# Sums taken up at the head of each four slots in a gather-and-sum loop

## The chip, the cores and the metric

The kernel runs on one core of a Trainium2 chip, in one launch. The metric is the time of one execution in microseconds. The kernel before was run three times: 5961.7, 5947.33 and 5960.33, with a median of 5960.33. The profile shows one more execution of it.

In the profile the engines are called PE (TensorE: matrix products), PEld (the load of the stationary operand, which overlaps PE), DVE (VectorE), ACT (ScalarE), POOL (GpSimd) and SP (the engine that starts most plain transfers). Each works through its own queue, and they wait for each other by semaphores.

## What is computed

A graph has 12,500 nodes with 256 features and 200,000 edges, and the edges come sorted by target. Three layers of mean aggregation run over it; a linear attention and a mixture of eight experts follow, and the kernel computes these too. The part around the change is this:

```python
def _sage_conv(x, src, dst, Wl, bl, Wr, num_nodes):
    msg = x[src]
    s = jax.ops.segment_sum(msg, dst, num_segments=num_nodes)
    cnt = jax.ops.segment_sum(jnp.ones((msg.shape[0],), x.dtype), dst, num_segments=num_nodes)
    agg = s / jnp.maximum(cnt, 1.0)[:, None]
    return agg @ Wl.T + bl + x @ Wr.T
...
h = _sage_conv(x, src, dst, Wl0, bl0, Wr0, n)
h = jax.nn.leaky_relu(h, LEAKY_SLOPE)
h = _sage_conv(h, src, dst, Wl1, bl1, Wr1, n)
h = jax.nn.leaky_relu(h, LEAKY_SLOPE)
h = _sage_conv(h, src, dst, Wl2, bl2, Wr2, n)
```

## The kernel before: slots, take-ups and what is woven between them

**Slots.** The sorted edges are cut into slots of at most 128 edges that all point into one block of 128 target nodes. There are 98 blocks, walked from the last to the first, so that the ones with few edges come first. For a slot, `gather` lets POOL start an indirect DMA that brings the 128 source rows into a message tile (`msgs`, a ring of `MSGS` = 32 tiles in the first two layers). `make_hots` lets DVE compare target numbers with a row of column numbers, for four slots at a time (`FEW` = 4); the result, `hots`, is a matrix of zeros and ones per slot. `product` multiplies the two on PE and adds the result to the sums of the slot's block. The sums (`acc`) lie in PSUM, in a ring of 4 blocks in the first layer (`layer` 0) and of 6 in the second. In the first layer the message tile has one column more, filled with ones, so that the last column of the sums is the count of edges. The first two layers take 1240 slots each in this way; the six densest blocks are summed by another way, from matrices of counts that DVE and PE build during the first layer (class `Counts`, lines 1115 to 1260: sorting by `MAX8` and `MATCH_REPLACE8`, then comparisons into `src_hot` and `dst_hot`, then products `p_n`). `MSGS` appears in the waiting steps of that counting too (`all_sorted`), beside its use as the ring's size.

**The loop of the first two layers** (after the return of the `if e` branch in `on_the_way_of`) does four slots per iteration. In the program's order an iteration at slot `s` is:

1. the four gathers (POOL);
2. the product of slot `s + 3` (PE), which waits for the youngest of the four messages;
3. `stage(0)`, one step of the work that follows finished sums (`products`: transposes, the two linear maps, their evictions by ACT and DVE), then `stage(1)`, one step of independent work (`first_products` in the first layer, `attended` in the second);
4. `make_hots` for slot `s + 12` (DVE, line 1374);
5. `take_up` of every block whose due slot is `s` (DVE, lines 1428 to 1438);
6. the loads of `h` that are due (`ask`);
7. the products of slots `s`, `s + 1`, `s + 2` (PE, line 1402), and after each of them one or two steps of the counting (DVE, PE and POOL) or, later, of the dense sums.

**take_up** reads a finished sum out of PSUM and clears it. In the first layer it has four instructions on DVE: the maximum of the count and 1 (line 1428), the reciprocal (1429), the scaling into the tile `mean` (1430) and the clearing of the sum (1438). Lines 1430 and 1438 are put into a group, `evicts`, on which products are told not to wait; line 1428, which also reads the sums, isn't put into it. The clearing is waited for by the first product of the next iteration (`cleared`, with `BACK` = 4). In the second layer a take-up is lines 1434 and 1438 alone, both in the group, and blocks are taken up in pairs. When the last block of a group is taken up, its `products` are appended to the queue `soon`, from which `stage(0)` draws.

**Reuse of tiles.** `hots` has `HOTS + 1` = 4 buffers of four slots in the pool `work`; the one for slot `s + 12` was last read by the products of the iteration before. `mean` has two buffers in the same pool. The gather of slot `s` (a multiple of 4) waits for the last product that reads the tile of slot `s - 32`. The third layer (`e` is set) has a loop of its own.

Of the kernel before, what the change touches and what calls it, by code (L numbers as in the profile page):

```python
# [41 lines left out]
F32 = mybir.dt.float32  # L42
BF = mybir.dt.bfloat16
# [12 lines left out]
P = 128  # L56
D = 256
# [5 lines left out]
G = 4  # L63
# [3 lines left out]
W = D + 1  # L67
AHEAD = 8
EARLY = 16
MSGS, PARTED = 32, 24  # L70
FEW = 4
HOTS = 3
BACK = 4
# [13 lines left out]
def gps_kernel(ctx: ExitStack, tc: tile.TileContext, x, src, dst, wlr, bl, wq, wk, wv,  # L87
# [15 lines left out]
    for r0, r1, most in ((0, SMALL, G), (SMALL, NB, 2)):  # L103
        for r in range(r0, r1, most):
            n = min(most, r1 - r)
# [169 lines left out]
    with ExitStack() as first:  # L275
        sort = first.enter_context(tc.tile_pool(name="sort", bufs=1))
        work = first.enter_context(tc.tile_pool(name="work", bufs=2))
        psum = first.enter_context(tc.tile_pool(name="psum1", bufs=1, space=PSUM))
# [27 lines left out]
        for c in range(NCH):  # L306
            s = slice(c * CW, (c + 1) * CW)
# [118 lines left out]
        for c in range(KC):  # L426
            n = min(P, NK - c * P)
# [591 lines left out]
    def open_pool(stack, name, **kw):  # L1019
        return stack.enter_context(tc.tile_pool(name=name, **{"bufs": 1, **kw}))  # L1020

    def take_messages(lists, n):

        msgs = [lists.tile([P, W], F32, name=f"msg{i}") for i in range(n)]
        for msg in msgs:
            nc.vector.memset(msg[:, D:], 1.0)
        return msgs
# [45 lines left out]
    def on_the_way():  # L1073


        with ExitStack() as stack:
            lists = open_pool(stack, "lists_w")
            work = open_pool(stack, "work_w", bufs=2)
            inv = lists.tile([P, NB], F32, name="inv_w")

            tables = [where, lists.tile([1, NS], I32, name="where1")]
            nc.vector.tensor_scalar(tables[1], where, 43.0, None, op0=OP.mult)
            nc.vector.tensor_scalar(tables[1], tables[1], 8, None, op0=OP.logical_shift_right)
            nc.vector.scalar_tensor_tensor(tables[1], tables[1], -float(RING[1]), where,
                                           op0=OP.mult, op1=OP.add)
            nc.vector.tensor_scalar(tables[1], tables[1], float(D), None, op0=OP.mult)
            nc.vector.tensor_scalar(where, where, RING[0] - 1, None, op0=OP.bitwise_and)
            nc.vector.tensor_scalar(where, where, 2.0 * D, None, op0=OP.mult)
            a = Attention(lists)
            stack.enter_context(tc.manual_schedule())  # L1090
            with ExitStack() as two:
                msgs = take_messages(open_pool(two, "messages"), MSGS)
                for layer in range(2):
                    with ExitStack() as own:
                        psum = open_pool(own, f"psum_w{layer}", space=PSUM)
                        on_the_way_of(layer, tables[layer], due[FEWER - 1], work, psum, inv, msgs,
                                      a, Counts(own), None)
            parted = open_pool(stack, "parted")
            msgs = [parted.tile([P, 3 * D], BF, name=f"msg_parts{i}") for i in range(PARTED)]
            psum = open_pool(stack, "psum_w2", space=PSUM)  # L1100
            e = Experts(open_pool(stack, "big"), work, psum)
            e.parted = parted
            nc.vector.tensor_scalar(where, where, 0.5, None, op0=OP.mult)
            c = Counts(stack)
            c.work = open_pool(stack, "sums2")
            on_the_way_of(2, where, due[MORE - 1], work, psum, inv, msgs, a, c, e)

    class Counts:
# [240 lines left out]
        def tile(self, shape, dtype, name, tag=None, bufs=None):  # L1349
            return self.pool.tile(shape, dtype, name=name, tag="any", bufs=self.bufs)  # L1350

    def on_the_way_of(layer, table, last, work, psum, inv, msgs, a, c, e):


        blocks = MORE if e else FEWER
# [4 lines left out]
        hots, made_of, cleared, taken, zs, at, at_of = {}, {}, {}, {}, {}, (), -1  # L1360
        rows_of = {}
        now, soon, later, made, left = [None, None], deque(), deque(), set(), {}
        whole = psum.tile([P, 2 * D], F32, name="whole", tag="whole")
        if layer == 0:
            psum = OneTag(psum, 3)
# [3 lines left out]

        def make_hots(s):  # L1370
            n = min(FEW, last - s)
            hot = (e.parted if e else work).tile([P, FEW, P], BF if e else F32, name="hots",
                                                 bufs=HOTS + 1)
            nc.vector.tensor_tensor(  # L1374
                hot[:, :n, :], cols.rearrange("p (o c) -> p o c", o=1).to_broadcast([P, n, P]),
                dst_of[:, s:s + n].rearrange("p (n o) -> p n o", o=1).to_broadcast([P, n, P]),
                OP.is_equal)
            for i in range(n):
                hots[s + i] = hot[:, i, :]
# [35 lines left out]
        def take_up(r, sums=None):  # L1415

            g = group_of[r]
            b, n = falling[g]
            j = NB - 1 - r - b
            by_slots = sums is None  # L1420
            if by_slots:
                sums = sums_of(r)
            if layer == 0:
                if g not in taken:
                    taken[g] = (work.tile([P, G, D], F32, name="mean") if by_slots else
                                c.work.tile([P, G, D], F32, name="mean_c"))
                if by_slots:
                    nc.vector.tensor_scalar(inv[:, r:r + 1], sums[:, D:], 1.0, None, op0=OP.max)
                    nc.vector.reciprocal(inv[:, r:r + 1], inv[:, r:r + 1])
                got = nc.vector.tensor_scalar(taken[g][:, j, :], sums[:, :D],  # L1430
                                              inv[:, r:r + 1], None, op0=OP.mult)
            else:
                h = zs[g][:, j, :]
                got = nc.vector.scalar_tensor_tensor(h, sums, inv[:, r:r + 1], h,
                                                     op0=OP.mult, op1=OP.add)
            if by_slots:
                tc.add_to_no_dep_group(evicts, got.ins)
            got = nc.vector.memset(sums, 0.0)
            if by_slots:
                tc.add_to_no_dep_group(evicts, got.ins)  # L1440
                cleared.setdefault(when[r] + BACK, []).append(got.ins)
            left[g] = left.get(g, n) - 1
            if left[g]:
                return
            h = zs.pop(g)
            if layer == 1:
                nc.vector.scalar_tensor_tensor(h[:, :n, :], h[:, :n, :], SLOPE, h[:, :n, :],
                                               op0=OP.mult, op1=OP.max)
            if layer < 2:
                soon.append([-1, products(layer, b, n, taken.pop(g, h), h, work, psum,  # L1450
                                          parts=c.work if layer else None), True])
            else:
                nc.sync.dma_start(rows(z_tab[2], b, n), h[:, :n, :])
                e.ready.append((b, n))
# [108 lines left out]
        for s in range(0, last, FEW):  # L1563
            for i in range(FEW):
                gather(s + i)
            product(s + FEW - 1)
            stage(0)
            share = SHARE[layer] * (2 if counting and c.sorting else 1)
            credit = min(credit + share, 2 * share)
            if credit > 0:  # L1570
                credit -= stage(1) or 0.0
            if s + HOTS * FEW < last:
                make_hots(s + HOTS * FEW)
            while r < blocks and when[r] == s:
                take_up(r)
                r += 1
            while g < len(z_by) and z_by[g] <= s:
                ask(g)
                g += 1
            if counting is None and summing is None:  # L1580
                pace = n_steps / ((sums_to - s) / FEW * (FEW - 1))
                nc.vector.memset(whole, 0.0)
                c.work = open_pool(c.stack, f"sums{layer}")
                for k in range(len(z_by), NG):
                    ask(k)
                summing = c.sums(layer, whole, take_up)
            for i in range(FEW - 1):
                product(s + i)
                if counting:
                    for _ in range(2 if i == 0 else 1):  # L1590
                        if counting and next(counting, 0) == 0:
                            counting = None
                elif summing:
                    due_steps += pace
                    while done_steps < due_steps:
                        next(summing, None)
                        done_steps += 1
            made_of[s + FEW - 1] = made_of[s + FEW - 2]
# [2 lines left out]
            r += 1  # L1601
        for _ in summing:
            pass
        while stage(0) is not None or stage(1) is not None:
            pass

# [54 lines left out]
```

## Time and profile before

| | us |
|---|---|
| three runs, lowest / median / highest | 5947.33 / 5960.33 / 5961.7 |
| the profiled execution, its time | 5964.23 |
| the same, from the first to the last instruction (span) | 5961.5 |

The mean granted clock of PE over the span is 0.95. By the starts of line 1402 in the timeline the first layer's slots run from 193 to 2125 us, the second layer's from 2149 to 3757; the third layer and the experts take the rest. The page counts busy time by engine, then shows 40 slices of 149 us, the DMA queues, the chain that ended last, and the costliest groups of instructions: line, engine, operation, tile, count, then busy time and mean duration, then how long the engine sat idle just before and what ended most of that.

### The profile page before, as it was taken

The page shows a single profiled execution, that of the slowest core. Times are in us where ns is not written, and L with a number is a line of the kernel's source. Part 1 is how long each engine was busy: PE and PEld are TensorE (multiplying, and loading weights), DVE is VectorE, ACT ScalarE, POOL GpSimd, SP SyncE. Part 2 cuts the span into 40 slices and gives each one's busy share as a digit, 9 for nine tenths or more (in the row PEclk, how much of TensorE's full clock was granted, in tenths as well). Part 3 has the DMA queues.
Part 4 walks back from the last instruction along what each step waited for, and adds up shares of the span by engine and source line. Part 5 has one row for each costly group of instructions (what it writes and reads, how often), then busy time and mean ns, then how long its engine had stood idle before and what let it go on. Part 6 is the DMA issues. An engine that isn't in the chain of part 4 may idle for free. (4 is left out here: it accounts for less than half of the span.)

```text
span 5961.5 us, 75064 instructions
## 1 busy us (share of the span) xinstructions
PE 5080.2 (85%) x23992; PEld 3751.7 (63%) x23992; DVE 2605.2 (44%) x7130; ACT 1058.4 (18%) x1970; POOL 4084.3 (69%) x4146
## 2 busy tenths in 40 slices
PE   1677899989899978878777776599999999999999
PEld 0456666666787856656655555366666666666667
DVE  6637768676322233333332222244444444444433
ACT  3211111212000000000000000032233223322333
POOL 1677676777677767777777777666666666666661
PEclk9989999999999989999988888699999999999999
DMA  6545454456788867767765555556566656655551
GB/s 200 164 132 167 152 151 138 145 161 184 229 262 258 258 188 249 232 223 249 223 211 179 184 172 156 182 172 191 175 182 183 186 168 182 183 172 173 166 160 50
DMA packets 712593, 1101.62 MB, mean 185 GB/s; under 512 B 105872, under 2 KB 551334, under 8 KB 711964
## 3 DMA queue, kind: packets, MB, share of 16 engines
q0 software_dynamic: 213712, 604.20, 34.9%
q1 hardware_dynamic: 480927, 472.47, 24.4%
q10 hardware_dynamic: 17578, 20.04, 1.0%
q8 instruction: 223, 3.65, 0.3%
q14 instruction: 153, 1.25, 0.1%
HBM read 908.22 MB, written 188.11 MB: 184 GB/s over the span
## 5 line engine op out<-in xcount | busy, mean ns | idle before, releaser
L1382 POOL DMA_INDIRECT msg<-y,src_of x2480 | 2522.9, 1017 | 886.0 <-issue 660.0
L1402 PE MATMUL acc<-msg,hots 128*128 128x257 f32 (+1 forms) x4960 | 1413.1, 411 | 566.6 <-DMA msg<-y,src_of 379.2
L1382 POOL DMA_INDIRECT msg_parts<-y_parts,src_of x1404 | 1405.1, 1001 | 689.9 <-issue 347.6
L1402 PEld LDWEIGHTS acc<-msg,hots 128*128 128x128 f32 x4960 | 959.4, 203 | 842.9 <-issue 459.5
L1374 DVE TENSOR_TENSOR hots<-cols,dst_of 128x512 f32<-128x512 f32 (+1 forms) x971 | 663.7, 687 | 1242.1 <-PE acc L1402 1241.5
L976 PE MATMUL p_h<-turned,w_sb 128*128 128x512 f32 (+1 forms) x1728 | 754.7, 561 | 37.8 <-ACT hT L978 37.8
L1331 PE MATMUL whole<-y_c,count 128*128 128x256 f32 x2744 | 738.9, 394 | 16.4 <-DMA y_c<-y 8.6
L945 PE MATMUL p_y<-w_sb,hT 128*128 128x256 f32 x3136 | 748.0, 382 | 1.2 <-DVE x L932 1.1
L1402 PE MATMUL acc<-msg_parts,hots 128*128 128x256 bf16 x4212 | 631.7, 277 | 32.4 <-DMA msg_parts<-y_parts,src_of 18.7
L1402 PEld LDWEIGHTS <-hots 128*128 128x128 bf16 x4212 | 415.5, 100 | 360.7 <-issue 258.9
L945 PEld LDWEIGHTS p_y<-w_sb,hT 128*128 128x128 f32 x3136 | 571.4, 192 | 70.7 <-DVE x L932 1.6
L1331 PEld LDWEIGHTS whole<-y_c,count 128*128 128x128 f32 x2744 | 539.6, 200 | 95.8 <-issue 17.1
L932 DVE SCALAR_TENSOR_TENSOR x<-p_y,comb,x 128x256 f32<-128x256 f32 x784 | 340.5, 476 | 445.9 <-PE p_y L945 445.7
L664 ACT COPY turned<-p_tr 128x512 f32<-128x512 f32 (+1 forms) x270 | 137.7, 550 | 1953.8 <-PE p_tr L662 1853.1
L978 ACT ACTIVATE hT<-p_h,b_sb 128x512 f32<-128x512 f32 (+1 forms) x432 | 276.8, 647 | 1167.1 <-PE p_h L976 1162.2
L976 PEld LDWEIGHTS p_h<-turned,w_sb 128*128 128x128 f32 x1728 | 302.5, 193 | 227.1 <-issue 173.1
L248 PE MATMUL p_mm<-wlr_sb,turned 128*128 128x512 f32 x784 | 356.1, 597 | 0.5 <-ACT turned L664 0.5
L258 DVE TENSOR_TENSOR yz<-p_mm,bl_sb 128x256 f32<-128x256 f32 x196 | 80.7, 423 | 515.8 <-ACT y L257 257.0
L1212 DVE TENSOR_SCALAR src_hot<-nums,source_of 128x384 bf16<-128x384 uint16 x693 | 224.3, 324 | 123.8 <-PE p_n L1232 123.7
L1232 PE MATMUL p_n<-dst_hot,src_hot 128*128 128x256 bf16 x2058 | 266.8, 279 | 0.4 <-DVE dst_hot L1214 0.4
L248 PEld LDWEIGHTS p_mm<-wlr_sb,turned 128*128 128x128 f32 x784 | 150.4, 192 | 149.0 <-issue 130.1
L1232 PEld LDWEIGHTS <-src_hot 128*128 128x128 bf16 x2058 | 202.7, 100 | 57.0 <-issue 11.3
(301 smaller groups left out, 3840.4 us busy)
## 6 DMA issues: line engine op xcount, KB each, us to landing
count<-counts SPq DMA_DIRECT2D x294, 256.0 KB
y_c<-y SPq DMA_DIRECT2D x294, 256.0 KB
msg<-y,src_of POOLq DMA_INDIRECT x2480
counts<-counts_sb SPq DMA_DIRECT2D x96, 384.0 KB
h<-z SPq DMA_DIRECT2D x66, 512.0 KB
z<-yz SPq DMA_DIRECT2D x98, 256.0 KB
msg_parts<-y_parts,src_of POOLq DMA_INDIRECT x1404
y_parts<-y SPq DMA_DIRECT2D x49, 384.0 KB
```

The costliest lines, as they stand in the source:

```text
L248: nc.tensor.matmul(p, hT[:, k, j * P:(j + 1) * P], w[:, k, :], start=(k == 0), stop=(k == 1))
L664: nc.scalar.copy(tT[:, k, :n * P], p_tr[:, :n * P])
L932: nc.vector.scalar_tensor_tensor(xt[:, j, :], p[:, j - j0, :], comb[:, j, i:i + 1], xt[:, j, :], op0=OP.mult, op1=OP.add)
L945: nc.tensor.matmul(p[:, j - j0, :], hT[:, k, j * P:(j + 1) * P], e.w2[:, i, k, :], start=(k == 0), stop=(k == 1))
L976: nc.tensor.matmul(p_h[:, :n * P], e.w1[:, i, k, m * P:(m + 1) * P], tT[:, k, :n * P], start=(k == 0), stop=(k == 1))
L978: nc.scalar.activation(hT[:, m, :n * P], p_h[:, :n * P], AF.Gelu, bias=e.b1[:, i, m:m + 1])
L1212: nc.vector.tensor_scalar(src_hot[:, i, :], self.nums, source[:, c:c + 1], None, op0=OP.is_equal)
L1232: nc.tensor.matmul(p[:, t, :], s_hot[:, (t0 + t) * P:(t0 + t + 1) * P], d_hot, start=(i == 0), stop=(i == len(mine) - 1))
L1331: nc.tensor.matmul(acc[:, h * D:(h + 1) * D], c[:, j, h * P:(h + 1) * P], y[:, j, :], start=False, stop=True, skip_group_check=True)
L1374: nc.vector.tensor_tensor(hot[:, :n, :], cols.rearrange("p (o c) -> p o c", o=1).to_broadcast([P, n, P]), dst_of[:, s:s + n].rearrange("p ...
L1382: got = nc.gpsimd.indirect_dma_start(out=msgs[s % held] if e else msgs[s % held][:, :D], out_offset=None, in_=y_parts if e else y_tab[laye ...
L1402: got = nc.tensor.matmul(sums, hot, msgs[s % held][:, k * D:k * D + w], start=False, stop=True, skip_group_check=True)
```

## The change

Five edits, all for the first two layers:

- `take_up` of the blocks due at `s` moves from after `make_hots` to right after the four gathers, so ahead of the product of slot `s + 3`.
- A new queue `fresh` keeps the follow-up work of a take-up out of `soon` until after that iteration's `stage(0)`.
- `hots` has `HOTS + 2` = 5 buffers in place of 4.
- `hots` and `mean` of these layers move from the pool `work` to a new pool `early` with two buffers by default, which is closed with the messages.
- `MSGS` is 28 in place of 32.

```diff
-MSGS, PARTED = 32, 24
+MSGS, PARTED = 28, 24
...
                 msgs = take_messages(open_pool(two, "messages"), MSGS)
+                early = open_pool(two, "early", bufs=2)
...
+        fresh = []
...
-            hot = (e.parted if e else work).tile([P, FEW, P], BF if e else F32, name="hots",
-                                                 bufs=HOTS + 1)
+            hot = (e.parted if e else early).tile([P, FEW, P], BF if e else F32, name="hots",
+                                                  bufs=HOTS + (1 if e else 2))
...
-                    taken[g] = (work.tile([P, G, D], F32, name="mean") if by_slots else
+                    taken[g] = (early.tile([P, G, D], F32, name="mean") if by_slots else
...
-                soon.append([-1, products(layer, b, n, taken.pop(g, h), h, work, psum,
+                fresh.append([-1, products(layer, b, n, taken.pop(g, h), h, work, psum,
...
             for i in range(FEW):
                 gather(s + i)
+            while r < blocks and when[r] == s:
+                take_up(r)
+                r += 1
             product(s + FEW - 1)
             stage(0)
+            soon.extend(fresh)
+            fresh.clear()
...
                 make_hots(s + HOTS * FEW)
-            while r < blocks and when[r] == s:
-                take_up(r)
-                r += 1
...
         for _ in summing:
             pass
+        soon.extend(fresh)
         while stage(0) is not None or stage(1) is not None:
```

More of the change, by code (lines that the diff above doesn't have):

```diff
@@ L1096, in on_the_way @@
                         on_the_way_of(layer, tables[layer], due[FEWER - 1], work, psum, inv, msgs,
-                                      a, Counts(own), None)
+                                      a, Counts(own), None, early)
             parted = open_pool(stack, "parted")
@@ L1350, in tile, with on_the_way_of @@
             return self.pool.tile(shape, dtype, name=name, tag="any", bufs=self.bufs)
-    def on_the_way_of(layer, table, last, work, psum, inv, msgs, a, c, e):
+    def on_the_way_of(layer, table, last, work, psum, inv, msgs, a, c, e, early=None):
         blocks = MORE if e else FEWER
```

## The prediction

> **What bounds the kernel now.** I read the page first, then the table of windows over the stages, then the waits of POOL, PE and DVE window by window, and last the timeline around single take-ups.
>
> The page gives each engine's share, and the two halves of a slot:
>
> ```profile
> PE 5080.2 (85%) x23992; PEld 3751.7 (63%) x23992; DVE 2605.2 (44%) x7130; ACT 1058.4 (18%) x1970; POOL 4084.3 (69%) x4146
> ...
> L1382 POOL DMA_INDIRECT msg<-y,src_of x2480 | 2522.9, 1017 | 886.0 <-issue 660.0
> L1402 PE MATMUL acc<-msg,hots 128*128 128x257 f32 (+1 forms) x4960 | 1413.1, 411 | 566.6 <-DMA msg<-y,src_of 379.2
> ```
>
> A gather holds POOL for 0.95 us when undisturbed (0.95 in the timeline, 1.017 in the mean), and 0.30 us of issue follow: 1.25 us per slot is the fastest pace that the gathers allow. The windows part the stages (columns after the window: its length, then busy us and instructions of PE, PEld, DVE, ACT, POOL, then PE's clock, DMA share and GB/s):
>
> ```profile
> 450.00:745.00 295.00, 245.00 (x1160) 191.60 (x1161) 232.92 (x434) 47.50 (x102) 206.25 (x204) 0.93 0.52 159
> 745.00:1043.00 298.00, 272.50 (x1715) 205.60 (x1713) 223.30 (x738) 52.06 (x110) 207.49 (x180) 0.98 0.48 145
> ...
> 2130.00:3757.00 1627.00, 1236.41 (x4645) 933.75 (x4645) 500.09 (x910) 96.57 (x248) 1235.26 (x1240) 0.90 0.66 207
> ```
>
> **The second layer is paced by POOL.** Its 1240 gathers in 1627 us are 1.31 us each, near the 1.25 floor, and PE waits there for messages: the waits of PE from 2831 to 3428 are led by
>
> ```profile
> PE acc L1402 <- DMA msg<-y,src_of: 134.7, 56, 6.4
> ```
>
> **The first layer is paced by PE until about 1640 us.** From 450 to 1640 us POOL waits for the ring to come free, and from 450 to 1527 us PE waits for DVE's take-up (two answers: POOL's waits, then PE's):
>
> ```profile
> POOL msg L1382 <- PE acc L1402: 107.4, 44, 8.3
> ```
>
> ```profile
> PE acc L1402 <- DVE inv_w L1428: 101.1, 52, 5.4
> PE acc L1402 <- DMA msg<-y,src_of: 5.3, 2, 3.8
> ```
>
> Messages cost PE only 5.3 us in that stretch, and nothing from 550 to 1527, where the same view lists no wait for them. So PE's lost time passes on whole. From 1640 on POOL runs at its own pace (2.8 us of waits for PE from 1639 to 1937), and at 2095 to 2122 PE waits 1.4 to 3.7 us for messages in each iteration: the layer's end is POOL's. What reaches the end is when PE, about 1640 us, lets POOL go.
>
> **The wait that the change touches.** Line 1428 isn't in the group that products may ignore, so the next product in program order waits for it. Now that is the product of slot s; after the change it is that of slot s + 3, at the head. DVE works in order, so line 1428 comes when everything ahead of it on DVE is done. Now these are the evictions of both stages and `hots`; in the change, the counting steps of the iteration before. The timeline of one take-up (PE and DVE rows):
>
> ```profile
> 493.79 0.81 PE L1402 MATMUL acc<-msg,hots 128*128 128x257 f32 x3
> ...
> 494.44 1.89 PE L740 MATMUL p_z<-wlr_sb,turned 128*128 128x256 f32 x8
> ...
> 497.34 0.68 DVE L1374 TENSOR_TENSOR hots<-cols,dst_of 128x512 f32<-128x512 f32 x1
> ...
> 497.94 1.32 DVE L1169 MAX8 packed<-got_runs 99x8 f32<-99x1118 f32 x1
> ...
> 499.37 1.31 DVE L1170 MATCH_REPLACE8 got_runs<-packed,got_runs 99x1118 f32<-99x1118 f32 x1
> ...
> 500.60 0.68 DVE L742 TENSOR_TENSOR z<-p_z,bl_sb 128x512 f32<-128x512 f32 x1
> 501.19 0.68 DVE L1374 TENSOR_TENSOR hots<-cols,dst_of 128x512 f32<-128x512 f32 x1
> 501.79 0.15 DVE L1428 TENSOR_SCALAR inv_w<-acc 128x1 f32<-128x1 f32 x1
> ...
> 502.00 1.23 PE L1402 MATMUL acc<-msg,hots 128*128 128x257 f32 x2 [4.45 <-DVE inv_w L1428]
> ```
>
> The products of the iteration before end at 494.17 (in the first row), while DVE still owes it a counting pair, done at 499.37 + 1.31 = 500.68. Today PE does the product of s + 3 and both stages (to 497.55) in the meantime and then waits 4.45 us. With the take-up at the head, line 1428 runs right after 500.68 and PE's first product starts at about 500.9 instead of 494.0: 6.9 us of waiting, and the stage work comes after it. The two DVE pieces no longer ahead (z 0.68, `hots` 0.68) are less than the PE work that loses its cover. The iteration ends 6.9 − 4.45 = 2.45 us later.
>
> **The sum over all take-ups.** For each of the 53 take-ups from 450 to 1527 us I took three times from the timeline: A, the end of the last product of the iteration before; B, the end of the last counting instruction (lines 1130 to 1260) or clearing that precedes the take-up's iteration on DVE; C, the present start of the product of s + 3. Line 1428 then starts at the later of A + 0.1 and B + 0.05, takes 0.15, and PE starts 0.05 later (as in the rows, 501.79 + 0.15 to 502.00). The wait is that less C. All 53 have counting work before them.
>
> | us | take-ups | PE's wait now | at the head |
> |---|---|---|---|
> | 450 to 745 | 17 | 40.2 | 66.2 |
> | 745 to 1043 | 13 | 24.4 | 31.0 |
> | 1043 to 1341 | 14 | 26.5 | 32.2 |
> | 1341 to 1527 | 9 | 10.5 | 12.1 |
>
> 101.6 become 141.5: **+39.9**. I take 8 of it back, by judgement: where no eviction lies in the iteration, `hots` and the next counting steps start on DVE when they do today although PE is later, so the next lateness is some tenths smaller. Bounds: recovery of nothing, or of 20. Before 450 us the same sum is 22.9 to 28.6, but PE waits 25.1 us for messages there, and at 460 us again 3.8, so it is absorbed. After 1527, with no counting left, waits fall from 13 to 4, but POOL sets the pace: nothing.
>
> **The clock.** The stall above was followed by half clock:
>
> ```profile
> 502.00:505.60 3.60, 3.60 (x9) 2.86 (x10) 3.40 (x6) 0.00 (x0) 2.83 (x3) 0.50 0.93 306
> ```
>
> Eight product instructions there took 3.80 us, against 1.90 in other iterations: 1.9 more. The Trainium skill (TensorE: Matmul & The Clock Gate, "What's actually happening" and "HAM oscillation — how this bites in real kernels") says that an idle window of about 3.4 us puts the clock to half, and asks for no longer gap. This speaks against longer stalls. By it, 7 waits of the table are over 3.4 us now and 14 at the head: 7 × 1.9 = 13 us. The trace is harsher: 2.39 us of idle PE before 633.0 already led to half clock, and of 21 waits of at least 2.0 us, 17 did; at the head 34 are that long: 13 × 0.8 × 1.7 (half of a 3.4 us window of the trace) = 18 us. Both assume PE is full in the window, which it isn't always. I take **12**, bounds 0 and 20.
>
> **28 messages.** POOL may be four slots less ahead. In the second layer PE trails POOL's issue by no more than 9 slots where I looked, every 40th slot: nothing. In the first layer it costs once, when PE releases POOL near 1640: 4 × 1.25 = **5**. With more returns to POOL's pace up to 15; a gain is excluded.
>
> **Five `hots`.** DVE's waits for `hots` buffers sum to 1241.5 us in the page, but only to 6.9 in the windows from 450 to 1527 (0, 1.0, 5.0, 0.9); elsewhere POOL hides DVE. Gain 0, at most 7.
>
> **The rest.** `fresh` leaves a by-slot group's first step where it was, in the next iteration. After the dense sums it comes one iteration later; PE waits for messages in each of the last iterations of both layers, which hides it (else 4 us per layer). 12 fewer empty counting steps (4 + 4 + 4, at four per iteration) bring counting three iterations forward and remove no work: 0, bounds ±5. Instructions, DMAs and the queue of SP are as before. In the second layer the pairs' lines 1434 and 1438 stand ahead of the evictions, some 1.5 us, under POOL's pace: 0. The third layer keeps its loop.
>
> Sum: 39.9 − 8 + 12 + 5 = 49. Against the profiled 5964.2 this is 6013; that execution lay 4 us above the median of the runs, so I say **6010**, slower by 0.8%. About 0.3%, 18 us, is what a measurement here can tell from no change.
>
> **Rivals.**
> - *Faster, the head is a good place (18%).* If DVE were on time when the products end, or the first product weren't held by line 1428 at all, each wait would fall to the floor of about 0.45 us (A + 0.1 + 0.15 + 0.05, with the 0.16 by which products overlap): 53 × 0.45 = 24. PE gains 101.6 − 24 = 77 us, up to 10 of clock besides, less 5 for the ring: about 5885. POOL's 107.4 us of waits leave room. It decides where DVE's median lateness B − A is under about 1 us; I read some 1.9 from 1043 to 1341 and 4 from 450 to 745. For it speaks that PE would no longer wait behind evictions and `hots`; against it, that counting stands right before the head, and that `src_hot` itself waits 123.7 us for PE's `p_n` in this stretch, so it can't come earlier.
> - *No change (8%), about 5964:* the longer waits are recovered in the next iterations, DVE being the true limit. DVE's 79% busy from 450 to 745 speaks for it. Against it: after the delayed head DVE must wait for the first product and the stages before it can evict, so it loses time too.
> - *Much slower (8%), 6050 to 6080:* full half-clock loss (20), no recovery (40), four returns to POOL's pace (20), and some counting pushed on.
>
> My own case has 66%, within 5985 to 6050. The range 5910 to 6065 holds it, no change, part of the faster side and of the last rival. Chances: faster 0.18, same 0.08, slower 0.74.
>
> **What would show it.** In the profile after: PE's wait for line 1428 now sits ahead of the product of s + 3, 140 us or so from 450 to 1600 instead of 101; more half clock there; POOL's wait for PE near 107 + 49; first-layer products ending about 2175 instead of 2125; the second layer still some 1610 us from first product to last. I am wrong if those waits fall under 60 us, if PE's first product starts ahead of line 1428, or if PE again waits for messages between 550 and 1500.

## The result and the profile after

The changed kernel takes 6019.59 us in the median of 4 runs (6011.46 to 6026.51), beside 5956.75 for the kernel before (5947.33 to 5961.7, 4 runs): a ratio of 1.011, 95% interval 1.0098 to 1.0122, or 63 us more. The profiled execution took 6026.51, its span is 6024.7, and the mean clock 0.946. The lines of `hots`, the gather, the product and the take-up's first instruction are now 1376, 1384, 1404 and 1430. Two later groups of runs met gaps on all engines, in the kernel before too (6609 and 6608 us there), so their times are set only against each other.

The page of the changed kernel, engines and the two halves of a slot:

```profile
PE 5101.4 (85%) x23992; PEld 3766.0 (63%) x23992; DVE 2601.8 (43%) x7126; ACT 1059.3 (18%) x1970; POOL 4097.8 (68%) x4146
...
L1384 POOL DMA_INDIRECT msg<-y,src_of x2480 | 2521.8, 1017 | 954.1 <-issue 653.7
L1404 PE MATMUL acc<-msg,hots 128*128 128x257 f32 (+1 forms) x4960 | 1416.1, 411 | 622.2 <-DMA msg<-y,src_of 407.8
```

No engine has more instructions of weight: what grew is PE's busy time (5080.2 to 5101.4) and the idle time ahead of gathers (886.0 to 954.1) and products (566.6 to 622.2). The waits say whose the idle time is. POOL from 450 to 1640 us, then PE from 450 to 1527:

```profile
POOL msg L1384 <- PE acc L1404: 174.7, 56, 11.6
```

```profile
PE acc L1404 <- DVE inv_w L1430: 142.0, 45, 8.5
```

POOL waits 67 us more for the ring, PE 41 us more for the take-up, and still hardly ever for messages (6.7 us, 5.3 before). The timeline shows the wait in its new place (PE and DVE rows; this is the take-up at slot 188, which follows the one shown before):

```profile
520.45 1.32 DVE L1170 MAX8 packed<-got_runs 99x8 f32<-99x1118 f32 x1
...
521.88 1.31 DVE L1171 MATCH_REPLACE8 got_runs<-packed,got_runs 99x1118 f32<-99x1118 f32 x1
...
523.11 0.15 DVE L1430 TENSOR_SCALAR inv_w<-acc 128x1 f32<-128x1 f32 x1
...
523.31 1.23 PE L1404 MATMUL acc<-msg,hots 128*128 128x257 f32 x2 [6.70 <-DVE inv_w L1430]
...
526.03 3.38 PE L1404 MATMUL acc<-msg,hots 128*128 128x257 f32 x8
```

A counting pair stands right ahead of line 1430, PE idles 6.70 us (4.15 before, at this take-up), and the eight product instructions at 526.03 take 3.38 us, at a granted clock of 0.56, where 1.90 is usual.

To compare equal work I took the stretch from the first product of the iteration at slot 160 (found by counting products in both timelines) to the last product of the first layer; PE has 8007 instructions there in both. The windows (length; busy us and instructions of PE, PEld, DVE, ACT, POOL; clock, DMA share, GB/s), before and after:

```profile
460.80:2125.00 1664.20, 1515.25 (x8007) 1178.68 (x8007) 914.70 (x2569) 222.15 (x484) 1209.90 (x1163) 0.97 0.62 190
```

```profile
471.10:2198.00 1726.90, 1539.44 (x8007) 1194.04 (x8007) 909.38 (x2562) 222.80 (x484) 1212.98 (x1160) 0.95 0.59 183
```

The stretch is 62.7 us longer, and it starts 10.3 us later (471.1 in place of 460.8): together the 73 us by which the layer's last product comes later. For the same instructions PE is busy 24.2 us longer and idle 38.5 us longer. The longer busy time goes with the lower clock, 0.95 in place of 0.97. Most of the added idle time (34.4 us) lies in the part up to slot 800, which takes in the whole counting. PE's waits for the take-up there, before (to 1579.9) and after (to 1652.7):

```profile
PE acc L1402 <- DVE inv_w L1428: 102.1, 54, 5.4
```

```profile
PE acc L1404 <- DVE inv_w L1430: 141.0, 46, 8.5
```

That is 38.9 us more, and a wait of `p_t` for the same line adds 4.0. At slot 800 the changed kernel is 72.8 us behind.

From there on little changes. The last product of the first layer ends at 2198.0 instead of 2125.0 (+73), that of the second at 3826.0 instead of 3757.1 (+69), and the span is 63 longer.

### The profile page after: what moved, and what is told of

Read it like the earlier page. It is cut to its first block, busy times and chain, and to the rows that moved or that the text cites. A ratio compares the mean times of both kernels' runs of the same rounds, so it can differ in the third digit from the quotient of the medians.

```text
span 6024.7 us, 75049 instructions
## 1 busy us (share of the span) xinstructions
PE 5101.4 (85%) x23992; PEld 3766.0 (63%) x23992; DVE 2601.8 (43%) x7126; ACT 1059.3 (18%) x1970; POOL 4097.8 (68%) x4146
## 3 DMA queue, kind: packets, MB, share of 16 engines
q0 software_dynamic: 213712, 604.20, 34.4%
## 4 chain that ended last, share of the span: by engine, by line
PE 37%; DMA 9%; POOL 8%; issue 5%; ACT 2%; DVE 1%; SPq 0%; DVEq 0%; ACTq 0%; POOLq 0%
PE acc L1404 10%; PE p_h L976 10%; PE p_y L945 9%; POOL msg L1384 8%; DMA msg<-y,src_of 6%; PE whole L1332 3%; PE p_mm L248 2%; DMA o<-z 2%; PE p_a L802 1%; PE p_b L893 1%; DMA out<-x 1%; PE p_tr L662 1%; PE p_r L848 1%; ACT ex L825 1%; POOL msg_parts L1384 1%
## 5 line engine op out<-in xcount | busy, mean ns | idle before, releaser
L1384 POOL DMA_INDIRECT msg<-y,src_of x2480 | 2521.8, 1017 | 954.1 <-issue 653.7
L1404 PE MATMUL acc<-msg,hots 128*128 128x257 f32 (+1 forms) x4960 | 1416.1, 411 | 622.2 <-DMA msg<-y,src_of 407.8
L1376 DVE TENSOR_TENSOR hots<-cols,dst_of 128x512 f32<-128x512 f32 (+1 forms) x971 | 653.6, 686 | 830.4 <-PE acc L1404 829.7
L248 PE MATMUL p_mm<-wlr_sb,turned 128*128 128x512 f32 x784 | 371.4, 619 | 0.6 <-ACT turned L664 0.5
L1436 DVE SCALAR_TENSOR_TENSOR h<-acc,inv_w,h 128x256 f32<-128x256 f32 x188 | 90.8, 483 | 352.7 <-PE acc L1404 349.2
```

Of the source, the lines that this page charges most:

```text
L248: nc.tensor.matmul(p, hT[:, k, j * P:(j + 1) * P], w[:, k, :], start=(k == 0), stop=(k == 1))
L1376: nc.vector.tensor_tensor(hot[:, :n, :], cols.rearrange("p (o c) -> p o c", o=1).to_broadcast([P, n, P]), dst_of[:, s:s + n].rearrange("p ...
L1384: got = nc.gpsimd.indirect_dma_start(out=msgs[s % held] if e else msgs[s % held][:, :D], out_offset=None, in_=y_parts if e else y_tab[laye ...
L1404: got = nc.tensor.matmul(sums, hot, msgs[s % held][:, k * D:k * D + w], start=False, stop=True, skip_group_check=True)
```

## The experiments

Each ratio is to the kernel before in the same group of runs.

| kernel | median us | before us | ratio, 95% interval |
|---|---|---|---|
| changed | 6019.59 | 5956.75 | 1.011, 1.0098 to 1.0122 |
| e1_move | 6013.55 | 5955.21 | 1.0099, 1.0082 to 1.0116 |
| e3_no_move | 5978.5 | 5955.21 | 1.004, 1.0026 to 1.0055 |
| e4_group_before | 5919.03 | 5955.21 | 0.9933, 0.9917 to 0.995 |
| e5_group_after | 5914.61 | 5955.21 | 0.9929, 0.9913 to 0.9946 |
| e2_ring | 6609.43 | 6608.93 | 1.0001, 0.9989 to 1.0013 |
| e7_ring_same_steps | 6592.14 | 6608.93 | 0.9988, 0.9962 to 1.0014 |
| e6_count_behind | 6525.11 | 6608.93 | 0.9873, 0.9851 to 0.9895 |
| e9_move_group | 6539.89 | 6608.93 | 0.9888, 0.9859 to 0.9918 |
| e2b_ring | 6606.04 | 6608.17 | 0.9994, 0.9975 to 1.0013 |
| e6b_count_behind | 6523.22 | 6608.17 | 0.989, 0.9845 to 0.9934 |
| e9b_move_group | 6522.74 | 6608.17 | 0.9879, 0.9858 to 0.99 |
| e10_all | 6546.83 | 6608.17 | 0.9916, 0.9894 to 0.9937 |

### The move alone, and everything but the move

`e1_move` is the kernel before with the move and `fresh`; ring, pool and `hots` buffers stay.

```diff
             for i in range(FEW):
                 gather(s + i)
+            while r < blocks and when[r] == s:
+                take_up(r)
+                r += 1
             product(s + FEW - 1)
...
                 make_hots(s + HOTS * FEW)
-            while r < blocks and when[r] == s:
-                take_up(r)
-                r += 1
```

> The move to the head alone, on the kernel before: 32 messages, four hots buffers, the old pool. Theory (PE's first product waits at the head for line 1428, behind the counting steps of the iteration before): nearly the whole loss, 6005 to 6025 us; PE's wait for inv_w about 140 us from 450 to 1600 us. Rival (28 message tiles take POOL's lead away): within 10 us of before. Rival (the pool and the five buffers): within 10 us of before.

58 us slower: the move carries most of the loss. PE's wait for the line is 125.9 us from 450 to 1527, somewhat under the 140 expected. The stretch of equal work, and in it the wait up to slot 800:

```profile
465.60:2171.60 1706.00, 1527.53 (x8007) 1188.75 (x8007) 916.02 (x2565) 223.02 (x484) 1214.23 (x1163) 0.96 0.60 185
```

```profile
PE acc L1403 <- DVE inv_w L1429: 128.3, 47, 6.7
```

The stretch is 41.8 us longer than before; the wait grew by 26.2 and PE's busy time by 12.3.

`e3_no_move` is the changed kernel with the take-up back behind `make_hots`; its follow-up work goes straight to `soon` again.

```diff
-            while r < blocks and when[r] == s:
-                take_up(r)
-                r += 1
             product(s + FEW - 1)
...
                 make_hots(s + HOTS * FEW)
+            while r < blocks and when[r] == s:
+                take_up(r)
+                r += 1
```

> The changed kernel with the take-up put back behind hots: 28 messages, five hots buffers, the new pool stay. Theory: 5 us over before for the ring, 5957 to 5970 us. Rival (ring or pools): 6000 us or more.

23 us slower, between the two expectations. The same two views of this kernel:

```profile
461.30:2146.80 1685.50, 1521.09 (x8007) 1180.51 (x8007) 908.51 (x2566) 222.00 (x484) 1221.02 (x1163) 0.97 0.61 188
```

```profile
PE acc L1404 <- DVE inv_w L1430: 115.2, 55, 6.4
```

The stretch is 21.3 us longer than before, and 13.1 of it is more waiting for the take-up, though that stands in its old place here. PE hardly waits longer for messages (8.1 us from 450 to 1527, 5.3 before). So a good part of what the other edits cost goes through the same wait; which of them lengthens it isn't shown. By the medians 58 and 23 are more than the 63 of both together, but over the stretch of equal work the parts add: 41.8 and 21.3 beside 62.7.

### The wait itself taken away

The line that reads the count joins the group which products don't wait for; the products then write only to blocks that aren't being taken up.

```diff
-                    nc.vector.tensor_scalar(inv[:, r:r + 1], sums[:, D:], 1.0, None, op0=OP.max)
+                    got = nc.vector.tensor_scalar(inv[:, r:r + 1], sums[:, D:], 1.0, None,
+                                                  op0=OP.max)
+                    tc.add_to_no_dep_group(evicts, got.ins)
```

`e4_group_before` does it in the kernel before, `e5_group_after` in the changed one.

> The kernel before with line 1428 put into the group that products don't wait for, as lines 1430 and 1438 are; the take-up stays in its old place. Theory (PE's waits for that line pass whole to the end of the first layer): PE's 101 us of waits between 450 and 1527 go, and some half clock with them; PE needs 80 to 100 us less there, POOL's 107 us of waits for the ring shrink as much: 5850 to 5890 us. Rival (DVE is the true limit there and PE merely meets it at another place): within 18 us of before, with PE's waits moved to evictions, hots or p_n.

> The changed kernel with the same line put into the group. Theory (the head costs only through the wait on that line): the head is harmless now, within 15 us of the kernel before with that line in the group (about 5880 us). Rival (the take-up's place in DVE's queue costs by itself, delaying evictions): stays 30 us or more above that one.

With the wait gone, the changed kernel is 105 us faster than it was (6019.59 to 5914.61), and level with the other: the intervals of e4 and e5 overlap. So the take-up's place in DVE's queue costs nothing that can be seen by itself; it costs through the wait on that one line. The ring, the buffers and the pool are in e5 too, so without the wait no cost of theirs is seen either. But both gain only about 40 us (36 and 41), half of what I expected. PE's waits from 450 to 1527, first of e4, then of e5, say why:

```profile
PE acc L1402 <- DVE acc L1439: 42.9, 21, 4.4
PE acc L1402 <- DMA msg<-y,src_of: 22.7, 11, 3.2
```

```profile
PE acc L1404 <- DMA msg<-y,src_of: 31.8, 13, 6.3
PE acc L1404 <- DVE acc L1441: 26.1, 8, 4.6
```

Two other waits take the place of part of the old one: that of the next head's product for the clearing of the sums, and that for messages, which means that POOL's own pace now binds at times. POOL's waits for PE are down to 41.5 us in e4 and 26.6 in e5 in that window: there is little more to win from PE.

### What stands ahead of the take-up

`e6_count_behind` keeps the wait, the ring, the pool and the buffers of the changed kernel, and changes the order while counting runs: the three products first, then the take-up due at the next head, then the counting steps.

```diff
-            for i in range(FEW - 1):
-                product(s + i)
+            ahead = counting is not None
+            for i in range(FEW - 1 if ahead else 0):
+                product(s + i)
+            while ahead and r < blocks and when[r] == s + FEW and s + FEW < last:
+                take_up(r)
+                r += 1
+            for i in range(FEW - 1):
+                if not ahead:
+                    product(s + i)
                 if counting:
```

> The changed kernel with one order more: while counting runs, the three products of an iteration come first, then the take-up of the next iteration, then the counting steps. PE still waits for the read of the sums, in the same place. Theory (it is the counting steps ahead of the take-up on DVE that make the head late): PE's wait falls from 142 us to 25 to 50 between 450 and 1527, and the time to 5910 to 5945 us. Rival (the take-up is late whatever stands ahead, for instance by the evictions): wait over 90 us, time over 5985 us.

> The changed kernel with the take-up ahead of the counting steps, again. Theory (the counting steps ahead of the take-up make the head late): PE's wait for line 1428's counterpart is 25 to 60 us between 450 and 1527 in place of 142, and the ratio 0.990 to 0.998. Rival: wait over 90 us, ratio over 1.004.

The ratios are 0.9873 and 0.989, a larger gain than either expectation had. The nearest thing to the kernel before that was profiled in these groups is the same kernel with 28 tiles (e2b below, level with it). PE's waits between slots 160 and 720, first e2b, then e6b:

```profile
PE acc L1402 <- DVE inv_w L1428: 110.0, 40, 13.7
```

```profile
PE acc L1404 <- DVE inv_w L1430: 42.7, 20, 7.0
```

With the counting behind it, the take-up is nearly on time: 42.7 us (42.1 in e6_count_behind). Over the same slots the changed kernel had this, and the kernel before 96.0:

```profile
PE acc L1404 <- DVE inv_w L1430: 138.6, 44, 8.5
```

So it was mainly the counting steps that made the head late. The changed kernel itself wasn't run in these groups, so the two are set side by side only by their own kernels before. The edit also takes the counting out from between the products in every iteration; how much of the ratio comes from that isn't separated, so it is the wait and not the ratio that shows the cause.

### The ring

`e2_ring` and its repeat `e2b_ring` change the number of tiles alone; `e7_ring_same_steps` keeps the counting's empty steps at those of 32 as well.

```diff
-MSGS, PARTED = 32, 24
+MSGS, PARTED = 28, 24
```

```diff
-                for _ in range(MSGS - FEW):
+                for _ in range(32 - FEW):
...
-                    for _ in range(MSGS if k else 0):
+                    for _ in range(32 if k else 0):
```

> The kernel before with 28 message tiles, nothing else. The changed kernel without the move lay 23 us over before, where the sum had 5 for the ring. Theory (the ring, with its four slots less of lead, costs all of that): 5970 to 5985 us. Rival (the five hots buffers or the new pool cost it): 5957 to 5963 us.

> The kernel before with 28 message tiles, but the counting keeps its waiting steps of 32 (28 + 32 + 32 empty steps), so that it runs in the same iterations as before. Theory (the lead of POOL is what costs): the same as with 28 tiles and fewer steps, within 8 us. Rival (counting that comes three iterations earlier meets the stages in a worse way): near before, 5957 us, while 28 tiles with fewer steps lie 15 us or more over it.

> 28 message tiles alone, again, beside a kernel before that takes about 5955 us (the earlier look had 6609 us for the kernel before too, with gaps on every engine that neither kernel explains). Theory (the ring costs what the changed kernel without the move lost): ratio 1.002 to 1.005. Rival (the five buffers and the pool cost it): ratio under 1.001.

No effect is seen in any of the three. This doesn't settle the 23 us of `e3_no_move`. In these groups POOL waits for PE far more (457.5 us of `msg` waits in e2b, 130.4 in the profile of before), so a lead of POOL may count for less there. With 28 tiles the counting also comes three iterations earlier, which can change what stands ahead of a take-up; `e7_ring_same_steps` undoes that, but in these groups alone. Whether the ring, the fifth `hots` buffer or the pool cost those 23 us stays open.

### Versions with the line in the group

`e9_move_group` is `e1_move` with the line in the group; `e9b_move_group` repeats it, and `e10_all` adds the order of `e6_count_behind`.

> The move to the head and the line in the group, with 32 message tiles and four hots buffers in the old pool. Theory (28 tiles still cost something where POOL is held): 5 to 20 us under the changed kernel with the line in the group, 5895 to 5910 us. Rival (with PE ahead the ring no longer matters, or five hots buffers help there): 5912 to 5925 us.

> The move with the line in the group, 32 message tiles, four hots buffers, again. Theory (28 tiles cost little once PE keeps up, and POOL's own pace is the floor): ratio 0.988 to 0.993, at or a little under the changed kernel with the line in the group (0.9929).

> Both cures together on the kernel before with the move: the line in the group, and the take-up ahead of the counting steps; 32 tiles, four hots buffers. Theory (with the wait on the line gone, what is left is the wait for the clearing at the next head, 26 to 43 us with the cure of the group alone, and an earlier take-up shortens that too; POOL's own pace limits the rest): ratio 0.985 to 0.992. Rival (nothing left to gain, POOL sets the pace): the same as the move with the line in the group, within 0.002.

e9 and e9b gain 1.1 and 1.2%. e10 gains 0.8%, so no gain of the second cure is seen where the wait is gone. These stand in other groups than e4 and e5, so I don't rank them against those two.

## Why the prediction was right, point by point

**The bound and the path: right.** What PE lost in the counting stretch passed to the end of the first layer: 72.8 us at slot 800, 73 at its last product (the forecast had some 50, 2175 in place of 2198). The second layer kept its length, 2221.0 to 3826.0 against 2149.2 to 3757.1 (1605 and 1608 us). POOL's wait for the ring is 174.7 us where 156 was forecast.

**The wait at the head: right in place, its size in part by luck.** The sum over take-ups gave 141.5; the profile after has 142.0 in the same window. But that sum is of the move alone, and the move alone has 125.9. The other edits, which the sum doesn't hold, have 115.5 without the move, against 101.1 before. Up to slot 800 the growth of 38.9 is the same as 26.2 (e1) and 13.1 (e3) together.

**The recovery of 8 us: hidden in the whole, seen in the move alone.** The take-ups' sum had 39.9 more; e1 has 26.2 more, so some 14 less, between the 8 taken and the bound of 20. That it is recovery of the kind described isn't shown.

**Before 450 us: put at nothing, and it cost.** The forecast let the longer waits be absorbed by those for messages. From 150 to 450 us the waits for the line grew from 21.8 to 30.1, those for messages only fell from 25.1 to 24.4, and slot 160 comes 10.3 us later (4.8 in e1).

**The clock: right for the move, too small for the whole.** I had 12 us, with 20 as the upper bound. For the same 8007 instructions PE's busy time grew by 12.3 in e1, but by 24.2 in the changed kernel. I counted one half-clock window for each wait that newly passed a limit; waits that were long already grew too (the longest from 5.4 to 8.5 us, 6.7 in e1). Whether that is the rest wasn't tried.

**The ring: 5 us, not confirmed.** e3 puts ring, buffers and pool together at 23 us, more through the wait for the take-up than through POOL's lead; the ring alone showed nothing in other groups.

**The five `hots`:** their waits fell from 1241.5 us to 829.7 in the page and no time came of it that can be seen; alone they weren't tried.

**The sum:** 49 us were forecast and 63 came. The move's own wait and clock came near their terms (26.2 for 31.9, 12.3 for 12). What was missing is the start before slot 160 (10 us) and what the other edits add in wait and clock; on the other side, 10 us of the first layer's 73 were gone again by the end of the span (4 in the second layer, 6 after it), which is within the spread of the runs (15 us in four). So the forecast was right by its mechanism, and the number came as near as it did partly because errors offset each other.

**The rivals.** The faster case named the right condition: once PE isn't held by the line (e5) or DVE is nearly on time (e6), the head is harmless. Its 5885 us was too bold, since I let 77 us of PE time pass whole: waits for the clearing and for messages took about half. "No change, DVE being the limit" fails as a whole by e1; but e4 has a piece of it, as a wait of 42.9 us for the clearing stands where 101.1 for the line were.

## What to carry to other kernels

Moving an instruction to an earlier place in the program moves it behind other work in its engine's queue: before moving it, list what stands ahead of it there at that moment, and what the engine that waits for it was doing meanwhile. Look at which instruction of a step carries the wait. Here it was a read one number wide per partition, left out of a group in which its neighbours were: grouping it gained 0.7%, where moving the whole step lost 1.0%. Price a longer stall of PE with the clock that follows it. And compare profiles over stretches with the same instructions, and each edit by itself: the right total can be a sum of terms that weren't forecast.

## What the runs showed of the hardware

Longer stalls of PE went with a lower clock and longer products: in e1, 26.2 us more of waits for the take-up went with 12.3 us more of busy time for the same 8007 PE instructions (clock 0.97 to 0.96), in the changed kernel 38.9 us (and 4.0 of `p_t`) with 24.2 us (0.97 to 0.95). That is roughly half as much again.

In the profile of before, waits for line 1428 between 2.0 and 3.4 us were mostly followed by half clock already (10 of the 14 of that length between 450 and 1527 us, counted with the records of the clock), which is shorter than the idle window that the prediction quotes. The stall of 2.39 us that ends at 633.01, for example: the granted clock from 633.74 to 637.16 is 0.50.
